# Edge attention of a graph network: the next chunk's logits and products put ahead of the scans where a run is complete

## Chip, cores and metric

The kernel runs on one core of one Trainium2 chip. The metric is the device time of one execution in microseconds (us); the time of a kernel is the median of several executions.

## What is computed

One layer of a graph network on 6250 nodes with 128 features and 200000 edges, which are sorted by their target node `dst`. The input goes through a layer norm and a relu, then through two rounds of message passing (`mesh_conv`), then through an edge attention with 8 heads of 16 features, whose result is projected, group-normed and added. The change concerns the attention alone. Cut to it, the reference is:

```
q = (h @ qw + qb).reshape(n, H, HD)
k = (h @ kw + kb).reshape(n, H, HD)
v = (h @ vw + vb).reshape(n, H, HD)
logits = (q[dst] * k[src]).sum(-1) * scale + (edge_attr @ ew + eb)
amax = segment_max(logits, dst)
pe = exp(logits - amax[dst])
ssum = segment_sum(pe, dst)
w = pe / clip(ssum[dst], 1e-06)
o = segment_sum(w[:, :, None] * v[src], dst)
o = group_norm(o.reshape(n, D) @ ow + ob, an_g, an_b)
x + (h + o)
```

## The kernel before

**Chunks.** The edges are cut into 196 chunks of 1024 edges (8 tiles of 128), walked from the last to the first. `pipeline(3, Stage())` takes the attention one chunk a step. In step n it fetches chunk n+2, makes the logits of chunk n and the products with q of chunk n+1, and sums the values of a chunk some eight to ten steps back into its nodes.

**Fetching.** `fetch` issues eight indirect gathers on POOL (line 314), one a tile, which bring k and v of the edges' source nodes into one of eleven buffers (`g`, `ge`, `gl` in the profile; chunk c uses buffer c modulo 11). SP issues the loads: the rows of q (`pk`, line 928), and every second chunk the comparison data (`rel`, line 914, and `ohT`, line 917). The first gather of a chunk carries a hold: `kept.seen = marks[back]` makes it wait for an instruction of PE that was noted at the start of an earlier step, the last one that PE had been given by then. It also waits until the values of the chunk that used the buffer before have been weighted.

**Logits.** `products` (line 1672) are 8 matmuls that give each edge its row of q and the edge bias in PSUM (`qe`, one buffer). `logits` then multiplies them by the gathered k on DVE (line 1687, two instructions), copies the bias out on ACT (`ebs`, line 1689), reduces over the features (line 1692) and adds the bias (line 1695). The next products can start when `ebs` has been copied out of `qe`. `compared` makes the one-hot matrix `ohT` on ACT (lines 940 and 941).

**Runs.** The segment maximum is taken for a run of chunks together: 4 chunks first, then 19 runs of 8, then short runs of 7 down to 2. Where a run is complete, the step is here called a run step. There are 26 of them in the part of the program that the change touches; the last steps, from 189 on, follow an order written out by hand, which does not change. `maxima` is a generator in pieces: the logits are transposed into PSUM (PE, line 1718, 8 transposes), two scans run over them on DVE (lines 1722 and 1725), the result is transposed back (PE, line 1729), and then the maxima are subtracted (line 1733), exponentiated (ACT, line 1735) and multiplied with a mask (line 1736). A call of `next` moves it on by one piece.

**Values.** `values` is a column copy on ACT (lines 1746, 1942, 1943) and the weighting on DVE (`weighted`, line 1750), which frees a gather buffer. `sums` (line 1757) are 8 matmuls with the one-hot `oh` (line 945). The sums of the chunk before are merged into the nodes in two parts: `merge` (lines 1790 to 1772: seven small instructions on DVE and two on ACT) and `add_late` in the next step (lines 1776 to 1782).

**The order in a run step.** `second` issues, around the sums of one chunk: the transposes, the one-hot, the addition, the sums, then by its third `next(mine)` the two scans and the transposes back, and then the merge. After it come `first` (the logits of chunk n), `finish` (the rest of `maxima`, and the weighting of the next chunk to be summed, which is one of the run just completed), `compared`, and the products of chunk n+1. Each engine works through its instructions in the order in which they are issued. In the run steps 4 and 12 no chunk is summed yet, so there all of `maxima` is issued by `finish`, behind the logits.

Of the kernel before, what the change touches and what calls it, by code (L numbers as in the profile page):

```python
# [41 lines left out]
EARLY = 3  # L42
# [25 lines left out]
def kernel(ctx: ExitStack, tc: tile.TileContext, x, src, dst, eat, w, out):  # L68
# [12 lines left out]
    NCH = -(-EI // TPC)  # L81
# [252 lines left out]
    def last_product():  # L334
        return next((i.name for i in reversed(nc.cur_bb.bb.instructions) if i.engine == mybir.EngineType.PE), None)
# [233 lines left out]
    def steps_of(i):  # L569


        ends, due, n = {}, {}, 0
        for m in spread(i):
            ends[n + m] = list(range(n, n + m))
            due.setdefault(n + m + (i == 3 or n < NCH - SOON), []).extend(ends[n + m])
            n += m
        waiting, todo, left = [], [], NCH
        while left:
            n = len(todo)
            waiting += due.get(n, ())  # L580
            steps = min([m for m in due if m > n], default=n + 1) - n
            k = -(-len(waiting) // steps)
            todo.append(waiting[:k])
            waiting = waiting[k:]
            left -= k
        return ends, todo
# [424 lines left out]
    def pipeline(i, stage, following=None, aside=iter(()), then=iter(())):  # L1011


        ends, todo = steps_of(i)
        starts = {n: j for j, (n, _, _) in enumerate(plans[i])}
        ahead = stage.ahead
        ks, under_way, said, marks = stage.ks, [], {}, []

        def go_on(n, those):
            for g in those:  # L1020
                if said.get(g) == "held" and n + 1 in ends:
                    continue
                said[g] = next(g, STOP)
                if said[g] is STOP:
                    under_way.remove(g)

        for c in range(ahead):
            if c not in ks:
                kept.seen = last_product() if c == stage.free else None
                ks[c] = stage.fetch(c)  # L1030
                kept.seen = None
                compared(ks[c])
            if c == 0:
                stage.products(ks[0])
        for n, seconds in enumerate(todo):
            if n == stage.ends:
                for g in under_way:
                    for _ in g:
                        pass
                stage.ending(ks, marks)  # L1040
                return
            new = None
            marks.append(last_product())
            if n + ahead < NCH and n + ahead not in ks:
                back = n - stage.lag(n + ahead)
                kept.seen = marks[back] if n + ahead >= stage.free and back >= 0 else None
                new = ks[n + ahead] = stage.fetch(n + ahead)
                kept.seen = None
            elif following and n + ahead >= NCH:
                kept.seen = last_product()  # L1050
                new = following.prefetch(n + ahead - NCH)
                kept.seen = None
            if n + 1 < NCH and stage.soon:
                stage.products(ks[n + 1])
            run = [ks[c] for c in ends.get(n, ())]
            stage.root(run)
            early = stage.soon and n > NCH - SOON
            if early:
                ahead_of = [g for g in under_way if said.get(g) not in ("var", "root")]
                go_on(n, ahead_of)  # L1060
            if new and stage.soon:
                compared(new)
            first = (lambda k: lambda: stage.first(k))(ks[n]) if n < NCH else None
            stage.then = [ks[c] for c in (todo[n + 1] if n + 1 < len(todo) else ()) if c in ks]
            if stage.second(run, [ks.pop(c) for c in seconds], first) and first:
                first()
            stage.finish()
            if new and not stage.soon:
                compared(new)
            if n + 1 < NCH and not stage.soon:  # L1070
                stage.products(ks[n + 1])
            if n + 1 < len(todo):
                stage.early(ks, n, todo[n + 1])
            if n in starts:
                for _ in aside:
                    pass
                under_way.append(stage.batch(starts[n]))
            go_on(n, [g for g in under_way if not early or g not in ahead_of])
            if n % 2 == 0:
                next(aside, STOP)  # L1080
            if next(aside, STOP) is STOP and n > min(starts):
                next(then, None)
            if n < NCH:
                stage.reduce(ks[n])
        if following:
            next(kept.rest)
        stage.flush()
        for g in (*under_way, aside, then):
            for _ in g:
                pass  # L1090
# [266 lines left out]
    def convs(general=False):  # L1357
        with ExitStack() as es:
# [78 lines left out]
                                         scale=mask[:, q, k.j:k.j + 1])  # L1437

            class Stage:
                ahead, soon, ends = 2, True, None  # L1440
                lag = staticmethod(lambda c: 0)

                def __init__(self, i):
# [184 lines left out]
    def attention(general=False):  # L1628
# [206 lines left out]
                    k.oh[:, t, :], iota_j, k.dm[:, t:t + 1], None, ALU.is_equal), behind)  # L1835

        class Stage:
            ahead, soon, free = 2, False, EARLY + 1
            lag = staticmethod(lambda c: 3 if c < 12 else 2 if c < 14 else 1 if c < 19 else 0)
            sums, late, nb = [], [], None  # L1840
            lg, j, both = None, 0, None
# [64 lines left out]
            def second(self, run, ks, first):  # L1906


                pieces = iter(())
                if run:  # L1910
                    pieces = maxima(run, self.lg, self.nb, self.bp)
                    self.nb = None
                for n, k in enumerate(ks):
                    mine = pieces if n == len(ks) - 1 else iter(())
                    next(mine, None)
                    if k.oh is None:
                        onehot(k, pools, iota_of(k))
                    if self.sums and self.sums[0].j >= ONE:
                        self.sums[0].win = wins[self.sums[0].j]
                    next(mine, None)  # L1920


                    if self.late:
                        add_late(self.late.pop(0))
                    if k.c > self.done:
                        self.values(k)
                    sums(k, VK + H + 1)
                    next(mine, None)
                    self.values_ahead(ks[n + 1:] or self.then)
                    if self.sums:  # L1930
                        self.merge(self.sums[0])
                        self.late.append(self.sums.pop())
                    self.sums.append(k)
                self.pieces = pieces
                return True
# [28 lines left out]
            ends = NCH - ENDS  # L1964
# [75 lines left out]
        if not general:  # L2040
            stage = Stage()
# [122 lines left out]
```

## Time and profile before

| what | value |
|---|---|
| median of 3 runs | 7012.45 us (7008.08 to 7033.32) |
| the profiled execution | 6977.15 us |
| its span, first to last instruction | 6975.4 us |
| mean granted clock of TensorE | 0.700 |
| busy: PE, DVE, ACT, POOL | 56%, 70%, 48%, 64% of the span |
| the attention | about 4640 us to the end |

A row of the timeline gives the start in us from the span's start, the duration, the engine, the line, the operation, `out<-in` by the program's names, the shape and a count; in brackets stand the idle time of the engine just before it and what ended that. Rows that differ in little are printed as one row with a count. "PEld" is TensorE's loading of weights, "SPq" are transfers issued by SP. In the order rows below a scan has the name SCALAR_TENSOR_TENSOR and the rows with ISA are small instructions of the loop's addressing.

### The profile page before, as it was taken

The page shows a single profiled execution, that of the slowest core. Times are in us where ns is not written, and L with a number is a line of the kernel's source. Part 1 is how long each engine was busy: PE and PEld are TensorE (multiplying, and loading weights), DVE is VectorE, ACT ScalarE, POOL GpSimd, SP SyncE. Part 2 cuts the span into 40 slices and gives each one's busy share as a digit, 9 for nine tenths or more (in the row PEclk, how much of TensorE's full clock was granted, in tenths as well). Part 3 has the DMA queues.
Part 4 walks back from the last instruction along what each step waited for, and adds up shares of the span by engine and source line. Part 5 has one row for each costly group of instructions (what it writes and reads, how often), then busy time and mean ns, then how long its engine had stood idle before and what let it go on. Part 6 is the DMA issues. An engine that isn't in the chain of part 4 may idle for free. (4 is left out here: it accounts for less than half of the span.)

```text
span 6975.4 us, 66960 instructions
## 1 busy us (share of the span) xinstructions
PE 3884.5 (56%) x20796; PEld 3580.4 (51%) x20797; DVE 4886.9 (70%) x6981; ACT 3365.8 (48%) x5296; POOL 4465.4 (64%) x4714
## 2 busy tenths in 40 slices
PE   5555554555555555555555555545555565555555
PEld 4555554554455555555555454544455555445554
DVE  6677777776767667676777777755666667667766
ACT  5555555555555555555555555532222223223465
POOL 4666666666666666666666666665666666666664
PEclk8666666777777666666677777766776767767677
DMA  4223323322232222222233333333444444444442
GB/s 123 75 73 83 102 74 85 80 75 79 77 81 76 65 71 68 70 71 67 69 88 88 84 89 85 88 99 99 119 120 115 119 118 125 120 122 115 118 119 81
DMA packets 384808, 640.95 MB, mean 92 GB/s; under 512 B 91440, under 2 KB 250652, under 8 KB 382827
## 3 DMA queue, kind: packets, MB, share of 16 engines
q0 software_dynamic: 175056, 410.03, 22.4%
q1 hardware_dynamic: 208170, 226.05, 11.5%
q8 instruction: 168, 2.75, 0.2%
q14 instruction: 198, 1.62, 0.1%
q10 hardware_dynamic: 1216, 0.49, 0.0%
HBM read 588.85 MB, written 48.48 MB: 91 GB/s over the span
## 5 line engine op out<-in xcount | busy, mean ns | idle before, releaser
L314 POOL DMA_INDIRECT g<-b_d,src_i x3078 | 2917.0, 948 | 1590.5 <-issue 861.5
L1431 PE MATMUL u<-h,oh 128*128 128x129 f32 (+1 forms) x6252 | 1363.5, 393 | 1573.9 <-issue 963.0
L1431 PEld LDWEIGHTS u<-h,oh 128*128 128x128 f32 x6252 | 1231.0, 294 | 1706.6 <-issue 1056.4
L314 POOL DMA_INDIRECT g<-kv_d,src_i x995 | 948.0, 953 | 552.6 <-issue 270.0
L1392 PE MATMUL m<-pk,ohT 101*128 101x128 f32 x6252 | 1054.2, 327 | 331.3 <-issue 315.5
L1392 PEld LDWEIGHTS m<-pk,ohT 101*128 101x128 f32 x6252 | 991.5, 243 | 355.6 <-issue 340.6
L1757 PE MATMUL us<-v,oh 128*128 128x145 f32 x3126 | 670.0, 374 | 527.3 <-issue 242.7
L1399 DVE TENSOR_TENSOR h<-m,g 128x1024 f32<-128x1024 f32 x392 | 474.3, 1210 | 695.1 <-remote 640.9
L1757 PEld LDWEIGHTS us<-v,oh 128*128 128x128 f32 x3126 | 591.7, 260 | 602.0 <-issue 370.4
L1672 PE MATMUL qe<-pk,ohT 101*128 101x136 f32 x3126 | 566.3, 351 | 264.2 <-ACT ebs L1689 193.1
L1423 ACT ACTIVATE h<-h 128x1024 f32<-128x1024 f32 (+2 forms) x394 | 413.0, 1048 | 568.5 <-issue 414.1
L1672 PEld LDWEIGHTS qe<-pk,ohT 101*128 101x128 f32 x3126 | 526.2, 252 | 302.8 <-ACT ebs L1689 217.7
L940 ACT ACTIVATE ohT<-rel,minus_p 96x1024 f32<-96x1024 bf16 x588 | 668.9, 1138 | 15.6 <-issue 11.3
L941 ACT ACTIVATE ohT<-ohT 96x1024 f32<-96x1024 f32 x588 | 619.9, 1054 | 18.8
L1403 DVE TENSOR_REDUCE var<-sq 128x64 f32<-128x1024 f32 x392 | 474.2, 1210 | 172.1 <-ACT sq L1401 78.8
L314 POOL DMA_INDIRECT ge<-kv_d,src_i x408 | 388.9, 953 | 230.5 <-issue 109.7
L945 DVE TENSOR_TENSOR oh<-cps,dm 128x1024 f32<-128x1024 f32 x392 | 474.3, 1210 | 75.3 <-remote 65.8
L1436 ACT ACTIVATE u<-u,mask 128x129 f32<-128x129 f32 (+1 forms) x688 | 230.6, 335 | 533.5 <-remote 480.6
L1421 DVE TENSOR_TENSOR h<-h,cps 128x1024 f32<-128x1024 f32 (+2 forms) x394 | 477.4, 1212 | 13.5
L1422 DVE TENSOR_TENSOR h<-h,cps 128x1024 f32<-128x1024 f32 (+2 forms) x394 | 477.4, 1212 | 13.5
L1418 DVE TENSOR_TENSOR h<-h,cps 128x1024 f32<-128x1024 f32 (+2 forms) x394 | 474.5, 1204 | 0.8
L1401 ACT ACTIVATE sq<-h 128x1024 f32<-128x1024 f32 x392 | 411.6, 1050 | 119.8 <-DVE h L1399 101.5
(332 smaller groups left out, 4399.4 us busy)
## 6 DMA issues: line engine op xcount, KB each, us to landing
rel<-rel_d SPq DMA_DIRECT2D x291, 384.0 KB
g<-b_d,src_i POOLq DMA_INDIRECT x3078
pk<-a_d SPq DMA_DIRECT2D x552, 46.0 KB
g<-kv_d,src_i POOLq DMA_INDIRECT x995
ohT<-in_eat_dram SPq DMA_DIRECT2D x291, 40.0 KB
ge<-kv_d,src_i POOLq DMA_INDIRECT x408
a_d<-n_o SPq DMA_DIRECT2D x24, 256.0 KB
kv_d<-n_o SPq DMA_DIRECT2D x24, 256.0 KB
```

What stands on the lines that cost most here:

```text
L314: h = nc.gpsimd.indirect_dma_start(out=g[:, t, :table_d.shape[1]], out_offset=None, in_=table_d, in_offset=bass.IndirectOffsetOnAxis(ap=k. ...
L940: nc.scalar.activation(k.ohT[:WN, :], k.rel, AF.Square, bias=minus_p[:WN])
L941: nc.scalar.activation(k.ohT[:WN, :], k.ohT[:WN, :], AF.Relu, bias=1.0, scale=-4.0)
L945: return nc.vector.tensor_tensor(k.oh[:, :k.nt, :], iota[:, None, :].to_broadcast([P, k.nt, P]), k.dm[:, :, None].to_broadcast([P, k.nt, P ...
L1392: nc.tensor.matmul(k.m[:, t, :], lhsT=lhs[:, t * P:(t + 1) * P], rhs=rhs, start=(j == 0), stop=(j == len(terms) - 1))
L1399: nc.vector.tensor_tensor(k.mt, k.m[:, :n], k.g[:, :n], ALU.add)
L1418: nc.vector.tensor_tensor(m4, m4, k.rs.rearrange("p (t g) -> p t g", g=H)[:, a:a + n, :, None].to_broadcast([P, n, H, HD]), ALU.mult)
L1421: nc.vector.tensor_tensor(mt, mt, over_edges(gam, n), ALU.mult)
L1422: nc.vector.tensor_tensor(mt, mt, over_edges(bet, n), ALU.add)
L1431: nc.tensor.matmul(k.u[:, 0, :wide(k)], lhsT=k.oh[:, t, :], rhs=k.h[:, t, :wide(k)], start=start and t == 0, stop=stop and t == k.nt - 1)
L1672: nc.tensor.matmul(k.qe[:, t // TB, at:at + DB], lhsT=lhs[:, t * P:(t + 1) * P], rhs=rhs, start=(j == 0), stop=(j == len(terms) - 1))
L1757: nc.tensor.matmul(k.u[:, :wide], lhsT=k.oh[:, t, :], rhs=k.v[:, t, :wide], start=(t == 0), stop=(t == k.nt - 1))
```

## The change

In the run steps of the attention two things move. The third `next(mine)` leaves `second`, so that the scans and the transposes back are issued by `finish`, behind the merge and the logits of chunk n. And the products of chunk n+1 are issued ahead of `finish`, so ahead of the transposes back. The note from which the hold of a gather is taken (`stage.mark`) is kept at the last of these products, as it was before, when they stood last in the step. `values_ahead` inside `second` is skipped for the last chunk of a run step, since the new values are not there yet. The two rounds of message passing share `pipeline` and keep their order (`stage.soon` is true there).

```diff
@@ pipeline
-            marks.append(last_product())
+            marks.append(stage.mark or last_product())
+            stage.mark = None
...
             first = (lambda k: lambda: stage.first(k))(ks[n]) if n < NCH else None
+            apart = bool(run) and not stage.soon and n + 1 < NCH
             stage.then = [ks[c] for c in (todo[n + 1] if n + 1 < len(todo) else ()) if c in ks]
             if stage.second(run, [ks.pop(c) for c in seconds], first) and first:
                 first()
+            if apart:
+                stage.products(ks[n + 1])
+                stage.mark = last_product()
             stage.finish()
             if new and not stage.soon:
                 compared(new)
-            if n + 1 < NCH and not stage.soon:
+            if n + 1 < NCH and not stage.soon and not apart:
                 stage.products(ks[n + 1])
...
@@ Stage.second
                     sums(k, VK + H + 1)
-                    next(mine, None)
-                    self.values_ahead(ks[n + 1:] or self.then)
+                    if n < len(ks) - 1 or not run:
+                        self.values_ahead(ks[n + 1:] or self.then)
                     if self.sums:
                         self.merge(self.sums[0])
```

On DVE, in one of the run steps of eight chunks, the rows from the second scan to the weighting of the maxima stood like this before (`fw` is the second scan's result, `nm` to `M` the merge, `g_22907` the gathered rows of chunk n, `l_28635` its reduced logits):

```order
L1722 SCALAR_TENSOR_TENSOR blk<-nbs,blk 64x1024
L1725 SCALAR_TENSOR_TENSOR fw<-nbe,blk 64x1024
L1790 SCALAR_TENSOR_TENSOR nm<-us_22910,nm_120 128x2
L1793 TENSOR_TENSOR cm<-us_22910,nm 128x16
...
L1768 COPY M<-mn 128x16
L1687 TENSOR_TENSOR g_22907<-qe,g_22907 128x6x128
L1687 TENSOR_TENSOR g_22907<-qe,g_22907 128x2x128
L1692 TENSOR_REDUCE l_28635<-g_22907 128x64
L1695 TENSOR_TENSOR lg<-l_28635,ebs 128x8x8
L1733 TENSOR_TENSOR lg<-lg,blk 128x512
L1736 TENSOR_TENSOR wl<-blk,ef 128x512
```

The same place in the changed kernel, whose lines in the attention have numbers higher by 5:

```order
L1795 SCALAR_TENSOR_TENSOR nm<-us_22910,nm_120 128x2
L1798 TENSOR_TENSOR cm<-us_22910,nm 128x16
...
L1773 COPY M<-mn 128x16
L1692 TENSOR_TENSOR g_22907<-qe,g_22907 128x6x128
L1692 TENSOR_TENSOR g_22907<-qe,g_22907 128x2x128
L1697 TENSOR_REDUCE l_28624<-g_22907 128x64
L1700 TENSOR_TENSOR lg<-l_28624,ebs 128x8x8
L1727 SCALAR_TENSOR_TENSOR blk<-nbs,blk 64x1024
L1730 SCALAR_TENSOR_TENSOR fw<-nbe,blk 64x1024
L1738 TENSOR_TENSOR lg<-lg,blk 128x512
L1741 TENSOR_TENSOR wl<-blk,ef 128x512
```

The merge and the logits, which stood between the scans and the subtraction of the maxima, now stand ahead of the scans, and nothing is left between the second scan and the subtraction.

On PE, at the same run step, before (`lg` and `fw` are transposed, `us` takes the sums, `qe` the products):

```order
L1672 MATMUL qe<-pk_855,ohT 128x136 x8
L1718 MATMUL blk<-ident,lg 64x128 x8
L1757 MATMUL us_22911<-v,oh 128x145 x8
L1729 MATMUL blk<-ident,fw 128x64 x8
L1672 MATMUL qe<-pk_853,ohT 128x136 x8
L1757 MATMUL us_22910<-v,oh 128x145 x8
```

And now:

```order
L1677 MATMUL qe<-pk_855,ohT 128x136 x8
L1723 MATMUL blk<-ident,lg 64x128 x8
L1762 MATMUL us_22911<-v,oh 128x145 x8
L1677 MATMUL qe<-pk_853,ohT 128x136 x8
L1734 MATMUL blk<-ident,fw 128x64 x8
L1762 MATMUL us_22910<-v,oh 128x145 x8
```

The products of chunk n+1 and the transposes back have changed places. The rows of ACT, POOL and SP stand in the same order as before; the hold of the first gather after a run step still names the last of these products, which now comes eight PE instructions earlier.

More of the change, by code (lines that the diff above doesn't have):

```diff
@@ L1439, in convs @@
             class Stage:
-                ahead, soon, ends = 2, True, None
+                ahead, soon, ends, mark = 2, True, None, None
                 lag = staticmethod(lambda c: 0)
@@ L1837, in attention @@
         class Stage:
-            ahead, soon, free = 2, False, EARLY + 1
+            ahead, soon, free, mark = 2, False, EARLY + 1, None
             lag = staticmethod(lambda c: 3 if c < 12 else 2 if c < 14 else 1 if c < 19 else 0)
```

## The prediction

> **What bounds the kernel now.** I read the busy shares first, then the windows by stage for the attention, then the timeline around the scans, since the change touches nothing else.
>
> ```profile
> PE 3884.5 (56%) x20796; PEld 3580.4 (51%) x20797; DVE 4886.9 (70%) x6981; ACT 3365.8 (48%) x5296; POOL 4465.4 (64%) x4714
> ```
> ```profile
> 4860.00:5700.00 840.00, 480.66 (x2459) 428.57 (x2457) 570.62 (x1190) 228.09 (x657) 547.73 (x580) 0.70 0.44 117
> ```
>
> The second row is a stretch of 840 us of the attention: busy time and instructions of PE, its weight loads, DVE, ACT and POOL, then the clock and the DMA share. No engine is full. DVE works 68% of it, but POOL's 580 gathers follow each other at a step of 1.25 us (0.944 each by 547.73/580, and an issue gap of 0.30 in the rows below), which is 722 us of the 840. So POOL runs but for some 118 us, 13 us a run of eight chunks. A change counts if it lengthens or shortens a stop of POOL. The timeline of one run step shows the stops:
>
> ```profile
> 5509.35 0.37 PE L1718 MATMUL blk<-ident,lg 128*64 128x128 f32 x1 [2.52 <-issue]
> 5511.44 0.37 PE L1718 MATMUL blk<-ident,lg 128*64 128x128 f32 x1 [1.73 <-issue]
> 5511.61 3.36 PE L1757 MATMUL us<-v,oh 128*128 128x145 f32 x16
> 5511.85 2.29 DVE L1722 TENSOR_TENSOR_SCAN blk<-nbs,blk 64x1024 f32<-64x1024 bf16 x1 [8.06 <-PE blk L1718]
> 5511.94 0.94 POOL L314 DMA_INDIRECT ge<-kv_d,src_i  x1 [3.37 <-PE blk L1718]
> 5514.17 2.28 DVE L1725 TENSOR_TENSOR_SCAN fw<-nbe,blk 64x1024 f32<-64x1024 bf16 x1
> 5516.38 0.13 DVE L1790 SCALAR_TENSOR_TENSOR nm<-us,nm 128x2 f32<-128x2 f32 x1
> 5516.60 0.68 PE L1729 MATMUL blk<-ident,fw 64*128 64x64 f32 x8 [1.63 <-DVE nm L1790]
> 5517.27 1.28 DVE L1687 TENSOR_TENSOR gl<-qe,gl 128x768 f32<-128x768 f32 x2
> 5518.96 1.27 PE L1672 MATMUL qe<-pk,ohT 101*128 101x136 f32 x4 [1.69 <-ACT ebs L1689]
> 5519.58 3.38 PE L1672 MATMUL qe<-pk,ohT 101*128 101x136 f32 x14
> 5519.91 0.23 DVE L1695 TENSOR_TENSOR lg<-l,ebs 128x64 f32<-128x64 f32 x1
> 5520.05 0.68 DVE L1733 TENSOR_TENSOR lg<-lg,blk 128x512 f32<-128x512 f32 x1
> 5520.71 0.95 POOL L314 DMA_INDIRECT ge<-kv_d,src_i  x1 [0.30 <-issue]
> 5521.70 1.22 DVE L1750 TENSOR_TENSOR v<-ge,pe 128x1024 f32<-128x1024 f32 x1 [0.37 <-ACT v L1746]
> 5523.70 0.94 POOL L314 DMA_INDIRECT ge<-kv_d,src_i  x1 [2.04 <-PE qe L1672]
> 5525.70 4.20 PE L1757 MATMUL us<-v,oh 128*128 128x145 f32 x16 [2.75 <-DVE flat L1782]
> 5530.27 0.32 SPq L914 DMA_DIRECT2D rel<-rel_d  x1
> ```
>
> PE is late with the transposes of the logits: they come with gaps of 1.7 to 2.5 us. Their end releases DVE (after 8.06 us of idling) and POOL (after 3.37) within 0.1 us. I call the start of the first scan T. The two scans end at T+4.60 (5514.17+2.28), the merge and the logits fill DVE to T+8.20, and L1733 follows without a pause. L1750 ends at 5522.92, T+11.07. POOL's next set starts 0.78 us behind that, 2.04 after its last gather. The page names the products (end 5522.96) as what released it, but L1750 frees the buffer for just this set and ends at the same moment. A second kind of run step tells which of the two counts:
>
> ```profile
> 6176.37 2.29 DVE L1722 TENSOR_TENSOR_SCAN blk<-nbs,blk 64x1024 f32<-64x1024 bf16 x1 [7.49 <-remote]
> 6179.15 0.94 POOL L314 DMA_INDIRECT ge<-kv_d,src_i  x1 [0.30 <-issue]
> 6181.12 1.08 PE L1729 MATMUL blk<-ident,fw 64*128 64x64 f32 x8 [9.63 <-issue]
> 6181.77 1.28 DVE L1687 TENSOR_TENSOR ge<-qe,ge 128x768 f32<-128x768 f32 x2
> 6184.55 0.68 DVE L1733 TENSOR_TENSOR lg<-lg,blk 128x512 f32<-128x512 f32 x1
> 6186.20 1.22 DVE L1750 TENSOR_TENSOR v<-g,pe 128x1024 f32<-128x1024 f32 x1 [0.37 <-ACT v L1746]
> 6188.20 1.26 POOL L314 DMA_INDIRECT g<-kv_d,src_i  x1 [8.11 <-DVE n_rec L1266]
> ```
>
> Here too POOL starts 0.78 us behind the end of L1750 (6187.42). The buffer is the gate in both, so the quantity to forecast is **when L1750 starts, counted from T**, and what lies between: subtraction, exponential and column copy take 1.65 us from L1733 to L1750 in both and do not change.
>
> How many steps are of which kind, the scans' groups tell (window 4860 to 5750, then 5750 to 6480, with the subtraction of the latter):
>
> ```profile
> L1722 DVE TENSOR_TENSOR_SCAN blk<-nbs,blk 64x1024 f32<-64x1024 bf16 x10 | 22.9, 2286 | 79.4 <-PE blk L1718 72.3 <-remote 7.1
> ```
> ```profile
> L1722 DVE TENSOR_TENSOR_SCAN blk<-nbs,blk 64x1024 f32<-64x1024 bf16 x8 | 18.3, 2286 | 43.6 <-remote 37.0 <-issue 4.7 <-PE blk L1718 1.9
> L1733 DVE TENSOR_TENSOR lg<-lg,blk 128x512 f32<-128x512 f32 x8 | 5.5, 684 | 8.5 <-remote 8.5
> ```
>
> 72.3/8.06 is nine steps of the first kind; eight are of the second. Two come before and six shorter ones after, 26 in all less one odd.
>
> **The change, part by part.** No instruction is added or removed. On DVE the merge (5516.38 to 5517.27, 0.89 us) and the logits (to 5520.05, 2.78 us), 3.67 us together, move from behind the scans to ahead of them. On PE the 8 matmuls of products go ahead of the transposes back. Nothing is issued on SP or POOL in another order, and no DMA moves, so SP's loads wait for what they waited for.
>
> *First kind, the scans.* DVE idles 8.06 us ahead of T, and the moved 3.67 us would be free if they could run there. They can't: the merge needs the sums of the chunk before and the logits the products before them, both on PE, and in the trace's semaphore events these are signalled at 5511.53 and 5511.69, T-0.32 and T-0.16, in the same burst as the transposes. The merge starts at about T-0.29, the scans at T+3.38 and end at T+7.98. Then DVE has nothing to do until the transposes back are there. What that wait costs, the run step of chunk 12 shows, where the logits stand ahead of the scans already:
>
> ```profile
> 4766.55 2.28 DVE L1725 TENSOR_TENSOR_SCAN fw<-nbe,blk 64x1024 f32<-64x1024 bf16 x1
> 4768.97 1.09 PE L1729 MATMUL blk<-ident,fw 64*128 64x64 f32 x8 [5.86 <-DVE fw L1725]
> 4770.10 0.69 DVE L1733 TENSOR_TENSOR lg<-lg,blk 128x512 f32<-128x512 f32 x1 [1.27 <-PE blk L1729]
> ```
>
> 1.27 us, of which 0.14 and 0.04 are handing over and 1.09 the transposes after 5.86 us of idling. With PE in work just before, they take 0.68 (5516.60), together 0.86. In the changed step the products run from the end of the sums (5514.97, T+3.12) for 4.00 us or less, to T+7.1, under 0.9 us ahead of the transposes, so I take 0.86 and L1733 at T+8.84 instead of T+8.20: **0.64 us later**, nine times, +5.8 us. The bounds are 0 (if the burst lets the merge go half a microsecond earlier) and 1.05 (cold transposes): 0 to +9.5. The shift passes to L1750, to POOL's set and so to all that follows, once a run.
>
> *First kind, the products.* They end at T+7.1 instead of T+11.1. POOL's hold on them goes, and what is late next is L1750, which was late with it already: 0. The scans, which now run beside them, take 2.29 us beside the sums (5511.85) and beside an idle PE (6176.37) alike: 0.
>
> *Second kind.* T comes late while POOL is still gathering, and DVE idles ahead of it long after the sums and products are signalled, so merge and logits fit in. L1733 can come at T+4.60+0.15+1.08+0.04 = T+5.87 instead of T+8.18, 2.3 us earlier, unless the signal of the transposes back is late. It is in half of the cases:
>
> ```profile
> 5986.45 0.95 POOL L314 DMA_INDIRECT g<-kv_d,src_i  x1 [0.30 <-issue]
> 5990.30 0.69 DVE L1733 TENSOR_TENSOR lg<-lg,blk 128x512 f32<-128x512 f32 x1 [5.97 <-remote]
> ```
>
> L1733 waits 5.97 us, though the transposes were long done, until 2.9 us after POOL's last gather (5987.40). Four of the eight are of this sort (8.5 us in all) and gain nothing. In the step at 6176 POOL's set ends at 6180.09, and 2.7 us later is 6182.8, so L1733 gains 1.7 of the 2.3. By the same rule and the semaphore events another gains 1.6, one 0.4, and one loses 0.2: -3.5 us. Bounds: 0 to 4 x 2.3 = -9.2.
>
> *The rest.* The steps 4 and 12 had this order of DVE already: 0. The six short ones have both kinds among them; between six first kinds (+4) and two second kinds (-5) I take 0.
>
> **Sum.** +5.8 - 3.5 = +2.3, between -14 and +14, on the profiled execution's 6977.15: 6979. The median of the runs is 35.3 higher (7012.45), so **7015 us**.
>
> *A rule against it.* Behind the transposes back PE now idles from about T+8.8 to the next sums at T+14.5, 5.7 us instead of 2.75, and the products beside them run without a gap behind the sums. Sums after the 2.75 us of idling took 4.20 us, those at 5533.12 below 2.25. The Trainium skill, "TensorE: Matmul & The Clock Gate", section "HAM oscillation — how this bites in real kernels", says that idle gaps of PE over about 3.4 us throw it back to half its clock, which is then paid again at every restart; the trace agrees in so far as the 4.20 us stand at a restart, but that gap was below its figure. By that rule the sum would be +13 us higher, as the rival of the cold PE has it below; by the rows, where the restart is cold already, it stays.
>
> **The rivals.** *The hold is the gate (faster).* If the page's name for the releaser is right, POOL starts 0.30 after its last gather: 1.74 us earlier (of 2.04) in nine steps, -16, and 7.8 earlier (of the 8.11 at 6188.20) in the four of the second kind where L1733 doesn't wait, -31: together -47, 6930 profiled, 6965 by the median. For it stands the page; against it that POOL follows L1750 by 0.78 in both kinds, also where the products' end (6187.46) isn't named.
>
> *The transposes back are caught (slower).* In the second kind they are signalled only when POOL pauses. If that befell the first kind, where POOL's set ends at 5521.66, they would be signalled 2.7 us later, at T+12.5 instead of T+8.84: +4.3 us against now, ten times, +43 us: 7020 profiled, 7055 by the median. It decides as soon as `rel` is loaded (L914) before the transposes back, since behind that load the gaps begin. Against it: the next load is at 5530.27, T+18.4.
>
> *A cold PE (slower, less).* The next stretch shows its price:
>
> ```profile
> 5529.70 2.73 PE L1672 MATMUL qe<-pk,ohT 101*128 101x136 f32 x16
> 5533.12 2.25 PE L1757 MATMUL us<-v,oh 128*128 128x145 f32 x16 [0.69 <-DVE flat L1782]
> 5535.14 0.94 POOL L314 DMA_INDIRECT g<-kv_d,src_i  x1 [1.75 <-remote]
> ```
>
> Products at 4.00 instead of 2.73 cost 1.3 us, and POOL waits 1.45 over its gap there, for something remote. If that is PE, ten times 1.3 is +13: 7028. That the change does not do what it says is excluded by the order of the instructions.
>
> **How the numbers follow.** Forecast 0.76, the hold 0.07, the caught transposes 0.09, the cold PE 0.08. A measurement of this kernel can tell about 0.5%, 35 us, from no change. The forecast and the cold PE lie within it but for the spread of single runs (7008.08 to 7033.32): 0.82 same; the first rival gives most of faster, 0.08; the second most of slower, 0.10. The range takes the terms' bounds (-14 to +14) and the cold PE (+13), and half the runs' spread either way: 6984 to 7045. The two outer rivals are left out.
>
> **What would show it.** In the first kind L1738 (now) should wait about 0.9 us, ended by L1734, and stand at 8.84 us behind the end of the late transposes; POOL's stop behind the set should be 2.7 instead of 2.04 and end 0.78 behind the weighting. In the second kind the scans should start with no idle time behind logits that ended long before. It is wrong if POOL's set starts before the weighting ends, or if the signal of the transposes back is late with POOL gathering in the first kind.

## The result and the profile after

The changed kernel takes **7083.4 us** (median of 6 runs, 7071.52 to 7099.89) against 7034.25 for the kernel before, in 6 runs: a ratio of 1.0084 (95% interval 1.007 to 1.0097), worked out over all the runs; the two medians alone give 1.0070, at the lower end of the interval. The forecast was 7015 with a range up to 7045; the time lies above it. The profiled execution takes 7079.05 us, with a span of 7077.2.

Where the time went, the starts of the scans tell, which mark the same chunk in both profiled executions:

| stretch (run steps) | before, us | after, us | difference |
|---|---|---|---|
| start to the scan of step 4 | 4687.7 | 4746.0 | +58.3 |
| 4 to 28 | 270.2 | 271.4 | +1.2 |
| 28 to 100, nine runs, the first kind | 831.7 | 867.2 | +35.5 |
| 100 to 156, seven runs, the second kind | 675.9 | 666.8 | -9.1 |
| 156 to the end | 510.0 | 525.8 | +15.8 |

The first stretch is code that the change doesn't touch. The changed kernel ran it in 4688.9 us on another chip (below), so the 58 us are taken as scatter between executions. The attention itself is 43.4 us longer, which is about what the medians differ by (49). In the nine runs the work is the same, so the windows of these stretches can be laid side by side, first before, then after (busy time and instructions of PE, its weight loads, DVE, ACT, POOL):

```profile
4957.80:5789.50 831.70, 482.18 (x2473) 431.42 (x2472) 573.17 (x1201) 232.15 (x662) 545.43 (x576) 0.70 0.44 119
```
```profile
5017.50:5884.60 867.10, 461.68 (x2462) 413.42 (x2461) 574.36 (x1201) 231.95 (x662) 544.75 (x577) 0.71 0.41 114
```

DVE and POOL work as long as before, and PE 20 us less: 35 us of pure waiting came in. The timeline of one of these run steps after, to be held against the one at 5511.85 before:

```profile
5591.95 0.16 DVE L1795 SCALAR_TENSOR_TENSOR nm<-us,nm 128x2 f32<-128x2 f32 x1 [7.91 <-remote]
5592.06 4.08 PE L1762 MATMUL us<-v,oh 128*128 128x145 f32 x16
5592.35 0.94 POOL L314 DMA_INDIRECT ge<-kv_d,src_i  x1 [3.51 <-PE blk L1723]
5595.66 2.28 DVE L1727 TENSOR_TENSOR_SCAN blk<-nbs,blk 64x1024 f32<-64x1024 bf16 x1
5595.93 2.37 PE L1677 MATMUL qe<-pk,ohT 101*128 101x136 f32 x16
5597.98 2.28 DVE L1730 TENSOR_TENSOR_SCAN fw<-nbe,blk 64x1024 f32<-64x1024 bf16 x1
5600.40 1.08 PE L1734 MATMUL blk<-ident,fw 64*128 64x64 f32 x8 [2.11 <-DVE fw L1730]
5601.10 0.94 POOL L314 DMA_INDIRECT ge<-kv_d,src_i  x1 [0.30 <-issue]
5603.80 0.69 DVE L1738 TENSOR_TENSOR lg<-lg,blk 128x512 f32<-128x512 f32 x1 [3.54 <-remote]
5605.45 1.22 DVE L1755 TENSOR_TENSOR v<-ge,pe 128x1024 f32<-128x1024 f32 x1 [0.37 <-ACT v L1751]
5607.45 0.94 POOL L314 DMA_INDIRECT ge<-kv_d,src_i  x1 [5.40 <-DVE v L1755]
5609.45 4.21 PE L1762 MATMUL us<-v,oh 128*128 128x145 f32 x16 [7.97 <-DVE flat L1787]
```

The merge starts in the burst of PE's signals, the scans 3.71 us behind it, the transposes back at once behind the scans, all as forecast. But the transposes end at 5601.48 and the subtraction starts at 5603.80: **2.3 us in which the work is done and DVE doesn't know it**, until 1.76 us behind POOL's last gather (5602.04). Counted from the start of POOL's set, the subtraction came at 8.1 us before, was forecast at 8.75, and comes at 11.45. POOL's next set still starts 0.78 us behind the weighting. It is so in all nine, by the group of the subtraction (before, window 4900 to 5750; after, 4960 to 5850):

```profile
L1733 DVE TENSOR_TENSOR lg<-lg,blk 128x512 f32<-128x512 f32 x9 | 6.1, 682 | 0.0
L1738 DVE TENSOR_TENSOR lg<-lg,blk 128x512 f32<-128x512 f32 x9 | 6.2, 688 | 31.9 <-remote 31.9
```

3.5 us of waiting each, where there was none before. In the second kind (window 5850 to 6590) the subtraction waits 1.3 us each, most of it for the transposes back at work:

```profile
L1738 DVE TENSOR_TENSOR lg<-lg,blk 128x512 f32<-128x512 f32 x8 | 5.5, 688 | 10.5 <-PE blk L1734 9.4 <-issue 1.1
```

### The profile page after: what moved, and what is told of

The parts are those of the page before. It is cut to its first block, busy times and chain, and to the rows that moved or that the text cites. A ratio compares the mean times of both kernels' runs of the same rounds, so it can differ in the third digit from the quotient of the medians.

```text
span 7077.2 us, 66985 instructions
## 1 busy us (share of the span) xinstructions
PE 3881.8 (55%) x20796; PEld 3578.1 (51%) x20797; DVE 4892.5 (69%) x6981; ACT 3361.0 (47%) x5296; POOL 4463.2 (63%) x4714
## 5 line engine op out<-in xcount | busy, mean ns | idle before, releaser
L1436 PE MATMUL u<-h,oh 128*128 128x129 f32 (+1 forms) x6252 | 1381.5, 395 | 1461.2 <-issue 1010.9
L1436 PEld LDWEIGHTS u<-h,oh 128*128 128x128 f32 x6252 | 1245.3, 297 | 1604.6 <-issue 1127.4
L1677 PE MATMUL qe<-pk,ohT 101*128 101x136 f32 x3126 | 532.6, 335 | 242.0 <-ACT ebs L1694 175.9
L1677 PEld LDWEIGHTS qe<-pk,ohT 101*128 101x128 f32 x3126 | 494.3, 238 | 281.0 <-ACT ebs L1694 201.9
```

Of the source, the lines that this page charges most:

```text
L1436: nc.tensor.matmul(k.u[:, 0, :wide(k)], lhsT=k.oh[:, t, :], rhs=k.h[:, t, :wide(k)], start=start and t == 0, stop=stop and t == k.nt - 1)
L1677: nc.tensor.matmul(k.qe[:, t // TB, at:at + DB], lhsT=lhs[:, t * P:(t + 1) * P], rhs=rhs, start=(j == 0), stop=(j == len(terms) - 1))
```

## Experiments

The chips turned out to be of two sorts, which has to be known to read the runs. A signal is here the semaphore event that tells the other engines that an instruction of PE has ended. On chips 3, 8, 11 and 15 the kernel before takes some 5960 to 5980 us: there nearly every signal of PE in the attention comes within 0.03 us of the end of its matmul (in the profile of the scans-only run below all 533), and from the scans of step 4 to those of step 156 POOL idles over 0.7 us once at most. This is a window of that run, 640 gathers at 1.25 us in 800 us:

```profile
4200.00:5000.00 800.00, 489.31 (x2720) 453.88 (x2720) 636.91 (x1331) 252.98 (x730) 605.32 (x640) 0.77 0.48 137
```

On chips 5, 6 and 9 it takes 6960 to 7022 us, as on the chip of the two kernels, and PE's signals are late at times. I call these **holding chips**. The chip of a run can't be chosen, so some kernels ran up to three times, and four of them never met a holding chip. No profile of the kernel before was kept on the chips of the experiments. Each ratio is to the kernel before on the same chip.

**Theories.** *Held signal, by age:* what PE finishes later than about 8 us after the start of an unbroken series of gathers is signalled only when the series is over. In the changed kernel's profile the transposes back that end 8.2 to 8.4 us behind that start were signalled within 0.04 us in five run steps and 0.25 and 0.32 us late in two (second kind), those at 8.7 to 9.1 us 2.3 to 2.8 us late (first kind). *Lost cover:* moved work is paid, since nothing fills the wait. *Products ahead:* the products in PE's queue make the transposes back late.

**The changed kernel again, on chip 6.** No edit.

> The changed kernel itself, beside the one before on the same chip. If this chip holds PE's signals back (before near 7010 us), held-signal theory: ratio 1.006 to 1.010, with the subtraction waiting 2.3 us or more behind the transposes back in the first kind of run step. If it does not (before near 5964 us, all signals out within 0.02 us): POOL's gathers follow each other without a stop, and the ratio is 0.999 to 1.002. Rival, lost cover: slower by 0.6 to 0.8% on either chip.

Ratio 1.0071 (1.0052 to 1.009). The loss is the change's, also on another holding chip. The waits are shorter here than in the first profile: the subtraction waits 2.0 us in five of the nine first-kind steps and 2.8 to 3.5 in four, and the nine runs take 849.2 us against 867.2. A run of the changed kernel on a chip that doesn't hold is missing.

**The changed kernel with a pause in POOL's series, on chip 8 and beside the last one on chip 6.** Two POOL instructions that rewrite a constant with itself stand between the fourth and the fifth gather of a run step's set, from step 20 on:

```diff
         for t in range(n):
...
+            if t == 4 and kept.pause:
+                for _ in range(2):
+                    kept.behind = follows(nc.gpsimd.tensor_scalar(
+                        iota_j, iota_j, minus_big[:, 0:1], None, ALU.max), kept.behind).ins
             h = nc.gpsimd.indirect_dma_start(
```

> The changed kernel, with two POOL instructions (about 0.8 us each, they rewrite a constant with itself) between the fourth and the fifth gather of the set that runs during the scans of a run step. Held-signal theory: the series is broken, the transposes back end about 2.5 us into the new one and are signalled at once; the subtraction comes 5.9 instead of 8.1 us after the first scan, POOL's stop behind the set shrinks from 5.1 to about 1.2 us, and the run takes 94.1 us instead of 96.3, ratio to before 1.003 to 1.005. Rivals (lost cover, cold PE, products ahead): POOL's work gets longer and nothing else changes, the run takes 96.3 us or more, ratio 1.008.

> The changed kernel with the pause of two POOL instructions in the middle of the set that runs during the scans. Where signals are held back, held-signal theory: the pause breaks the series, the run of eight takes 94.1 us instead of 96.3, ratio 1.003 to 1.005. Where they are not: 26 pauses of 1.6 us are paid in full, 1.0075 as in the run before. Rivals: never better than the changed kernel.

Chip 8: 1.0078 (1.0061 to 1.0095). That is the number recorded for the rivals, but no signal is late on this chip, so it says nothing between them: the pauses are paid. Chip 6: **1.0036** (1.0023 to 1.0049), half of the loss gone by giving POOL more to do. The nine runs take 841.4 us against 849.2 in the execution without the pause on that chip. The timeline with it:

```profile
5514.98 1.30 POOL L316 TENSOR_SCALAR iota_j<-iota_j,minus_big 128x128 f32<-128x128 f32 x2
5518.27 1.08 PE L1739 MATMUL blk<-ident,fw 64*128 64x64 f32 x8 [2.14 <-DVE fw L1735]
5519.02 0.95 POOL L318 DMA_INDIRECT ge<-kv_d,src_i  x1 [0.30 <-issue]
5519.40 0.69 DVE L1743 TENSOR_TENSOR lg<-lg,blk 128x512 f32<-128x512 f32 x1 [1.27 <-issue]
5520.28 0.95 POOL L318 DMA_INDIRECT ge<-kv_d,src_i  x1 [0.31 <-issue]
```

The subtraction starts 0.04 us behind the transposes, with POOL gathering on, and 5.87 us behind the first scan, where 5.9 was expected. It is so in all nine steps; on the same chip without the pause it came 0.8 to 2.7 us behind them. The group of the subtraction, first without the pause, then with it (window 4860 to 5750; the second has one step more):

```profile
L1738 DVE TENSOR_TENSOR lg<-lg,blk 128x512 f32<-128x512 f32 x9 | 6.2, 687 | 23.4 <-remote 13.2 <-PE blk L1734 10.2
```
```profile
L1743 DVE TENSOR_TENSOR lg<-lg,blk 128x512 f32<-128x512 f32 x10 | 6.9, 688 | 10.4 <-PE blk L1739 6.6 <-issue 3.8
```

So the late signal hangs on POOL's unbroken series. Lost cover and a late PE are refuted as the main cause, since PE and DVE have the same order in both kernels. What is left of the loss includes the price of the pauses; it was not taken apart.

**Only the scans late (three runs, chips 8, 15 and 11).** The products go back behind the transposes back:

```diff
-            if apart:
-                stage.products(ks[n + 1])
-                stage.mark = last_product()
...
-            if n + 1 < NCH and not stage.soon and not apart:
+            if n + 1 < NCH and not stage.soon:
```

> Only the scans and the transposes back go behind the merge and the logits; the products of the next chunk stay behind the transposes back, as before. Held-signal theory (what PE signals later than about 8 us after the start of an unbroken series of POOL's gathers reaches the others only 1.7 us after the series' end, or 3 us after one of 16): the transposes back still end about 9 us into the set, so the subtraction waits as in the changed kernel, a run of eight takes 96.3 us instead of 92.3 in the stretch of the first kind, and the ratio to before is 1.006 to 1.009. Rival, products ahead (the products in PE's queue make the transposes back late): the run goes back to 92.3 + 0.6 us and the ratio to 1.001.

> Only the scans and the transposes back behind merge and logits, products as before. Where signals are held back (before near 6960 to 7035 us), held-signal theory: the transposes back end some 9 us into the set and wait for its end all the same; ratio as for the changed kernel, 1.005 to 1.009. Rival, products ahead: 1.001. Where signals are not held (before near 5964 us): 1.001 again.

> Only the scans and the transposes back behind merge and logits, products as before; sought is a chip that holds PE's signals back (before near 6960 to 7035 us). There, held-signal theory: the transposes back still end about 9 us into the set and wait for its end, ratio 1.005 to 1.009. Rival, products ahead: 1.001. On a chip that doesn't hold them: 1.001 as twice.

1.001 (1.0001 to 1.002), then 1.0013 and 1.0011: none fell on a holding chip. The 1.001 is the number recorded for the products-ahead rival in the first run, but no signal is late on these chips, so it tells nothing between the theories, only that where POOL doesn't stop this order costs at most 0.2%.

**Only the merge ahead (chips 8, 15 and 11).**

```diff
                     sums(k, VK + H + 1)
-                    next(mine, None)
...
                         self.late.append(self.sums.pop())
+                    next(mine, None)
```

> Only the merge (0.89 us) goes ahead of the scans; logits and products stay as before. Held-signal theory: the transposes back end 5.9 us into POOL's set and are signalled at once; the logits fill the wait, the run takes 92.3 us or up to 0.3 less, ratio 0.998 to 1.001. Rival, lost cover (whatever goes ahead of the scans is paid in full, 4.05 us a run for 3.67 us moved): 0.98 us a run, 93.3 us, ratio 1.002.

> Only the merge ahead of the scans. Where signals are held back, held-signal theory: the transposes back end 5.9 us into the set, signalled at once, ratio 0.998 to 1.002. Rival, lost cover: 0.98 us a run, 1.003 or more. Where they are not held: 1.000 again.

> Only the merge ahead of the scans; sought is a chip that holds PE's signals back. There, held-signal theory: the transposes back end 5.9 us into the set, signalled at once, 0.998 to 1.002. Rival, lost cover: 1.003 or more. On a chip that doesn't: 1.000 as twice.

0.9998 (0.9989 to 1.0008), 1.0002, 0.9999, none on a holding chip. Likewise **the changed order in the late runs alone** (`apart` only for steps 100 to 156), on chip 15:

> The changed order only in the run steps 100 to 156, the order of before in all others. Where signals are held back, held-signal theory: those steps gain up to 2.4 us each, as they did between the two profiled executions (runs of 94.1 instead of 96.5 us), the others lose nothing: ratio 0.997 to 0.999. Rival (the changed order costs wherever it stands): 1.001 to 1.003. Where signals are not held: 1.000.

1.0002 (0.9992 to 1.0011), as expected where signals are not held. And **the kernel before with a short pause ahead of every set**, on chips 15 and 3:

> The kernel before with one POOL instruction of about 0.65 us ahead of every set of gathers from step 20 on, so that no two sets run on in one series. Where signals are held back: if so short a pause breaks a series, the transposes of the logits and the holds are signalled in time, and the five stops of a run (12.3 us) give way to eight pauses (5.2 us): a run of eight takes 86 to 90 us, ratio 0.98 to 0.99. If it is too short to break it: 1.002 to 1.006. Where signals are not held, the pauses are paid: 170 sets by 0.65 us are 110 us, ratio 1.018.

> The kernel before with one POOL instruction of 0.65 us ahead of every set of gathers from step 20 on. Where signals are held back: if so short a pause breaks a series, the stops of a run (12.3 us) give way to eight pauses (5.2 us), a run takes 86 to 90 us, ratio 0.98 to 0.99. If it is too short: 1.002 to 1.006. Where they are not held: 1.017 as before.

1.017 (1.0153 to 1.0187) and 1.0173: the pauses are paid. Whether they would help a holding chip was not seen.

**Only the logits ahead (chips 8 and 15, then 5).** The merge stays behind the scans, the products behind the transposes back:

```diff
                     sums(k, VK + H + 1)
+                    if run and n == len(ks) - 1 and first:
+                        first()
+                        first = None
                     next(mine, None)
```

> Only the logits (2.78 us) go ahead of the scans; the merge stays behind them, the products stay behind the transposes back. Held-signal theory: the transposes back end 7.9 us into POOL's set, at the edge, where signals of before still came through at up to 8.5 us: the run takes 92.3 us (0.9998 to 1.002) if it is sent, 95.7 us (1.005) if it is held; in no case anything between. Rival, lost cover: 2.78 of 3.67 of the loss, 95.4 us, ratio 1.006, with a subtraction that waits for nothing that POOL ends.

> Only the logits (2.78 us) ahead of the scans, the merge and the products behind as before; sought is a chip that holds PE's signals back (before near 6960 to 7035 us). In the profiled executions there, transposes back that ended 8.1 to 8.4 us after the start of a set were signalled within 0.04 us, those that ended at 8.7 to 9.1 us only 1.2 to 2.8 us later. Held-signal theory: without the merge ahead of them they end at 7.8 to 8.2 us, on the early side; the subtraction waits at most 0.4 us behind the merge, the first kind of run takes the time of before up to +0.3, the second gains up to 1.7 us: ratio 0.997 to 1.001. Rival, lost cover: 2.78 of 3.67 of the changed kernel's loss, 1.004 to 1.006. Where signals are not held: 1.001 as before.

> Only the logits ahead of the scans; sought is a chip that holds PE's signals back (before near 6960 to 7035 us). Held-signal theory: the transposes back end 7.8 to 8.2 us into the set, on the early side of 8.4 to 8.7, ratio 0.997 to 1.001. Rival, lost cover: 1.004 to 1.006. Where signals are not held: 1.001 as twice.

1.0012 and 1.001 on the two chips that don't hold; on chip 5, which holds, **1.0036** (1.0023 to 1.0048). The held signal had expected less; the lost cover's 1.004 lies in the interval. The timeline there shows what it had left out:

```profile
5466.64 0.94 POOL L314 DMA_INDIRECT g<-kv_d,src_i  x1 [3.44 <-PE blk L1718]
5473.93 1.08 PE L1729 MATMUL blk<-ident,fw 64*128 64x64 f32 x8 [3.51 <-DVE nm L1790]
5474.95 3.99 PE L1672 MATMUL qe<-pk,ohT 101*128 101x136 f32 x16
5475.05 0.69 DVE L1733 TENSOR_TENSOR lg<-lg,blk 128x512 f32<-128x512 f32 x1 [0.38 <-issue]
5476.72 1.22 DVE L1750 TENSOR_TENSOR v<-g,pe 128x1024 f32<-128x1024 f32 x1 [0.37 <-ACT pe L1735]
5479.21 0.94 POOL L314 DMA_INDIRECT g<-kv_d,src_i  x1 [2.86 <-PE qe L1672]
```

The transposes back are signalled at once, as the held signal wants, and the subtraction waits 0.38 us behind the merge. What is left is another wait: the products, last on PE, end at 5478.94, and POOL starts 0.27 us behind them and 1.27 behind the weighting. In this step the hold on the products is the gate, which the change removes. From one set to the next POOL takes 12.57 us here, 11.76 in the kernel before (5511.94 to 5523.70): nine such steps would be 7 of the 26 us by which the medians differ. The rest was not taken apart.

**The merge behind the scans, the products ahead (chip 3 twice, then 9).** This was to join both: in time, and no hold.

```diff
+            def logits_and_products():
+                first()
+                stage.products(ks[n + 1])
+                stage.mark = last_product()
+            stage.both_ahead = logits_and_products if apart else None
...
+                    elif self.both_ahead:
+                        self.both_ahead()
+                        self.both_ahead = None
+                        next(mine, None)
```

> The changed kernel with the merge put back behind the scans: logits, scans, merge, subtraction on DVE, the products still ahead of the transposes back. Sought is a chip that holds PE's signals back (before 6960 to 7035 us). There, held-signal theory: the transposes back end 8.1 to 8.4 us into the set, in time, and the products no longer hold POOL as they did with the logits alone ahead (its set began 12.6 us after the one before, 1.28 behind the weighting); now 12.1 us, 0.78 behind the weighting, against 11.75 in the kernel before. First kind +0.3 us a run, second kind up to -2: ratio 0.998 to 1.001, so 0.89 us of merge decide over nearly all of the loss. Rival, lost cover: the bubble is filled by 0.89 of 3.67 us only, 1.005 or more. Where signals are not held: 1.001.

> The changed kernel with the merge behind the scans; sought is a chip that holds PE's signals back (before 6960 to 7035 us). There, held-signal theory: transposes back in time at 8.1 to 8.4 us into the set, POOL's next set 12.1 us after the one before and 0.78 behind the weighting: ratio 0.998 to 1.001. Rival, lost cover: 1.005 or more. Where signals are not held: 1.001 as before.

> The changed kernel with the merge behind the scans, on a chip that holds PE's signals back if this is one: ratio 0.998 to 1.001 by the held-signal theory, 1.005 or more by the lost cover. On another: 1.001 as twice.

1.0009 and 1.0014 on chip 3; on chip 9, which holds, **1.0077** (1.0057 to 1.0098), as much as the changed kernel lost. The held signal in the form "by age" falls here:

```profile
5495.22 0.94 POOL L314 DMA_INDIRECT g<-kv_d,src_i  x1 [3.50 <-remote]
5502.52 0.68 PE L1738 MATMUL blk<-ident,fw 64*128 64x64 f32 x8 [1.91 <-DVE nm L1799]
5503.96 0.95 POOL L314 DMA_INDIRECT g<-kv_d,src_i  x1 [0.31 <-issue]
5506.71 0.69 DVE L1742 TENSOR_TENSOR lg<-lg,blk 128x512 f32<-128x512 f32 x1 [3.46 <-remote]
```

The transposes back end 8.0 us into the set, earlier than with the logits alone ahead (8.4), and are held for 3.5 us all the same.

**What tells them apart is a count.** In PE's order the two kernels differ, up to the transposes back, in one thing: the products stand between. The windows from the start of POOL's set to the end of the transposes back give the instructions of PE in them (the two figures behind x, matmuls and weight loads). Before, first kind, and to the end of the products:

```profile
5511.94:5517.28 5.34, 3.71 (x24) 3.38 (x23) 5.20 (x9) 0.04 (x1) 4.12 (x5) 0.80 0.28 82
5511.94:5522.96 11.02, 7.70 (x40) 7.05 (x39) 10.37 (x16) 2.72 (x10) 7.58 (x8) 0.65 0.34 99
```

The changed kernel, first and second kind:

```profile
5592.35:5601.48 9.13, 7.02 (x40) 6.67 (x39) 7.70 (x10) 0.59 (x4) 7.00 (x8) 0.69 0.31 91
5882.07:5890.47 8.40, 6.50 (x30) 5.68 (x29) 6.98 (x6) 0.27 (x2) 6.57 (x7) 0.50 0.32 96
```

The logits alone ahead:

```profile
5466.60:5475.05 8.45, 4.94 (x25) 4.50 (x24) 7.80 (x12) 0.59 (x4) 6.58 (x7) 0.50 0.33 97
```

The merge behind and the products ahead, first and second kind:

```profile
5495.22:5503.21 7.99, 6.07 (x38) 5.76 (x37) 7.71 (x12) 0.40 (x4) 6.16 (x7) 0.77 0.31 91
5881.00:5889.41 8.41, 6.34 (x30) 5.53 (x28) 7.82 (x12) 0.59 (x4) 6.53 (x7) 0.50 0.32 97
```

With 47, 59, 49 and 58 instructions since the set's start the signal came within 0.04 us where something waited for it (in the kernel before nothing did, and the semaphore events have it at once where they have it); with 79 and 75 it was held for 2.3 and 3.5 us. In the 26 run steps of each of the six profiled executions on holding chips there are 58 transposes back that end within a series with 64 instructions or fewer behind its start and are waited for: 55 were signalled within 0.32 us. In two of the other three PE was still late from the series before; the third stands behind a stop of POOL of only 1.03 us, with 99 instructions behind the start of the set ahead of that stop. Of the 47 with 75 or more, none was signalled in less than 0.82 us. The five between have all sorts of delays. In the second kind part of the sums had run before the set began, which brings the same order of instructions to 59, so the products alone, without the count, don't make the signal late. The granted clock of the windows goes with the holding as well, 0.69 and 0.77 where the signal was held and 0.50 where it was not; but in the kernel before, two like steps at 0.69 and 0.78 have the semaphore event 0.02 us behind the end.

So the theory that stands: on a holding chip some 65 to 75 instructions of PE pass freely from the start of an unbroken series of gathers; what they signal later is held back, in the runs of eight chunks until the series breaks or ends. In six of the shorter, late run steps such signals came 1.2 to 4.8 us late, but 7 to 10 us ahead of the end of a series of sixteen gathers, so its end is not the only thing that lets them through. The theory was formed from these executions and was not tested by one of its own. That the late signal hangs on the unbroken series is shown by the pause; that the count decides and not something that goes with it is argued from the six traces. What in the chip does it stays open, so does why some chips don't, and whether the recording of the profile has a part in it was not tested.

## Why the prediction was wrong

**The step that failed** is the one of the first kind that said of the wait behind the scans: "0.14 and 0.04 are handing over", and so took 0.86 us from the scans to the subtraction. It supposed that DVE hears of the transposes back as soon as they end. They did end where it said (in six of the nine steps 0.68 us long, in the one shown 1.08, within its bound), but are heard of 2.3 to 2.8 us later. So the subtraction, and with it POOL's next set, comes 2.7 us later than forecast in each of the nine. A late signal of the transposes back in the first kind was the sign that I had named for being wrong. The moved order goes with it, as the six traces have it: with the products ahead, the transposes back are the 79th instruction of PE in POOL's set instead of the 47th. In the kernel before, the products were the ones held (they end at 5522.96, their signal comes 0.36 us later), where it cost nothing, since POOL waited for the weighting until then anyway.

**The rival that came true** is the caught transposes, to which I gave 0.09. It put the subtraction at T+12.5 and the price at +4.3 us a run; the subtraction came at about T+11.5 (1.75 us behind POOL's last gather, where 2.7 was taken), and the runs of the first kind grew by 35.5/9 = 3.9. It was priced for ten steps and nine are of that kind. So the price is nearer than its parts. The mechanism was right, the condition was wrong: it was to decide when `rel` is loaded before the transposes back, and no such load stands there (the last comes nearly 20 us earlier in the changed kernel). What I had read as following the load goes with PE's count in POOL's series.

**What held.** L1750 frees the buffer and POOL starts 0.78 us behind it, before and after: the gate was named rightly, and the rival that the hold on the products binds is refuted for the kernel before: with the products long done, POOL still starts 0.78 us behind the weighting. With the logits alone ahead it does bind, when the products end 3.9 us behind the subtraction's start. The merge starts in the burst of the signals and 3.7 us are added ahead of the scans. The scans take 2.28 us beside the products, which themselves took 2.37 us and not up to 4.00, so PE stood idle for 2.11 us ahead of the transposes back instead of under 0.9. The second kind gains, 9.1 us over its seven runs where I took 3.5, at the end of my bounds: most of them wait now 1.27 us for the transposes back, with 57 to 61 instructions behind the start of POOL's set. A cold PE costs nothing more in the step shown: the sums behind the longer idling, 7.97 us, took 4.21 us against 4.20.

**What was mis-sized.** The tail was taken as 0 and lost 15.8 us; its steps mix both kinds, and I have not taken them apart. The sum of the terms, with 2.7 us more for each of nine first-kind steps (+24), the second kind (-6 more) and the tail (+16), comes to about +36 us of the 43.4 measured. The range, too, doesn't add up from what it is said to hold: 7012.45-14-12.6 is 6986 and 7012.45+14+13+12.6 is 7052, not 6984 and 7045. The measured time lies above both ends.

**On the clock.** The Trainium skill, "TensorE: Matmul & The Clock Gate", section "HAM oscillation — how this bites in real kernels", has PE at half its clock behind idle gaps above about 3.4 us. All nine gaps ahead of the transposes back were shorter than that. In six steps, behind gaps of 2.25 to 3.13 us, they took 0.68 us; in three, behind gaps of 1.75 to 2.11 us, 0.79 to 1.08. The trace agrees in the six and not in the three, and the 0.4 us at most that it costs in a step is not what decided.

## What to carry to other kernels

Before moving work of one engine ahead of a step that another engine waits for, count what then stands ahead of it since the last pause of the traffic beside it, and look in the trace whether signals come when the work ends: the end of an instruction and the start of the one that waits for it are two different things. A price that a rival has, found in one part of the trace (in the kernel before, a signal that came 2.9 us behind POOL's last gather), should be explained before it is given a small chance. And a loss of this kind is a matter of the chip: on four of the seven chips of the experiments no signal was late, and the kernels that moved the same work ahead of the scans lost 0.14% at most.

## What the runs showed of the hardware

- The same program, the kernel before, takes 5963 to 5978 us on some chips, at a mean granted clock of 0.75 to 0.76, and 6960 to 7034 us on others, at 0.70 to 0.71. From the scans of step 4 to those of step 156 POOL idles over 0.7 us at most once on the former and 96 to 101 times on the latter.
- On the latter, PE's signals and then its instructions come late while POOL gathers without a pause. Then gaps of 1 to 2.5 us stand between PE's instructions, as in the quoted transposes of the logits. From the scans of step 4 to those of step 156 there are 169 to 187 gaps of over 0.6 us between two matmuls of one group, nine of ten of them 80 instructions or more behind the start of a series; on the other chips there are 3 or 4.
- A stop of 1.5 us between two gathers, with a pause of 1.3 us in it, let the signals through again; behind one of 1.03 us a signal was held. Signals held in a set of eight gathers came 0.3 to 1.8 us behind its last gather, in a series of sixteen mostly 2.6 to 3.1 us.
